# Score rows and A^T without TensorE in a two-layer graph kernel on Trainium2

## The chip, the cores and the metric

The kernel runs on one core of a Trainium2 chip. The metric is the device time of one execution in microseconds (us); the time before is the median of three runs. TensorE (PE) multiplies matrices and writes to PSUM. VectorE (DVE) and ScalarE (ACT) do elementwise work. GpSimd (POOL) and SyncE (SP) issue DMAs here; each engine runs its own instructions in order.

## What is computed

128 graphs of 128 nodes with 512 features each go through two layers; all data is float32. From the reference, shortened:

```python
h = maximum(layernorm(x), 0)                       # layer 0, X = h, A = adj
Xw = X @ Wv + bv
sj, si = Xw @ aw[:d, 0], Xw @ aw[d:, 0]
e = leaky_relu(sj[:, None, :] + si[:, :, None] + ab[0], 0.2)
alpha = A * exp(e)
T = alpha / (sum(alpha, axis=-1, keepdims=True) + 1e-12)
H = 0; Xk = X
for k in range(3):
    H = H + Xk @ Wk[k] + bk[k]
    Xk = einsum('bij,bjd->bid', T, Xk)
x = x + relu(H)

h = maximum(layernorm(x), 0)                       # layer 1
q, k = split(h @ Wqk, 2, axis=-1); v = h @ Wv
agg = einsum('bij,bjd->bid', adj, k * mask[:, :, None])
w = inv_scale * mask * einsum('bid,bid->bi', q, agg)
x = x + softmax(w, axis=1)[:, :, None] * v
```

## The kernel before, in words

**Tiles.** A round of the main loop handles two graphs (G = 2), so there are NP = 64 pairs. Nodes lie on the 128 partitions. `loads` holds x (`xg`) and the adjacency (`ag`), `front` and `late` the working tiles, `ps_m` four PSUM banks for the large products and `ps_t` four for everything else on TensorE.

**Layer 0** of pair p. `norm0` (L240) normalizes x into h; `by_blocks` (L258) writes h to DRAM (`hd`) and reads it back with its blocks exchanged (`hv`), so that VectorE's transpose, which turns blocks of 32x32, gives the whole transpose of h (`begin`, L447, by `transposed` L268). `score_sums` (L248) makes two dot products for each node, sj and si, by four VectorE operations with an accumulator (L255). `attention` (L274) needs sj along the free dimension, the same row on all partitions: `spread` (L95) lets TensorE transpose the column, broadcast to 128x128, into PSUM (L97). VectorE and ACT then make z, exp, the row sums and T (L280 to L294). TensorE also transposes A there (L298), and ACT scales it by the mask into `aT` (L302), for layer 1. `t_transposed` (L304) makes T^T on TensorE (L309), copies it, and multiplies it by T into (T^2)^T (L313). `propagate` (L317) gives T h and T^2 h in transposed form (L325). `prepare0` (L354) makes the sums of blocks that Strassen's scheme needs, and `strassen0` (L360) the product of [h, Th, T^2h] with the three weights in seven half-size products. They are called P1, P6, P7, P5, P2, P3, P4 here, in this order, by the first number in the calls of `product` (L340); each has 12 matmuls.

**Layer 1** of the pair before. `strassen1` (L387) multiplies h2 by a matrix of scores (Wq Wk^T) and by Wv in seven products of four matmuls, with the same names. It uses three PSUM banks a, b, c: P6 fills b, L398 reads b, and P5 writes b again. `aggregate` (L411) multiplies A by h2 (L417) and makes the scores w (L420). `finish` (L426) spreads w over the partitions as `attention` does (L97), makes the softmax over the nodes, scales v, adds it to x1 and stores the result.

**Order.** The main loop (L475 to L512) lets `strassen0` of pair p take in work of the next pair by two callbacks: `steps[0]` after P6 (begin, attention of p+1, finish of p-2) and `steps[1]` before P2 (t_transposed of p+1). After that come propagate of p+1, normalization of the new x1 into h2, strassen1 of p-1, aggregate of p-1, prepare0 of p+1, the transpose of h2 into X2, and last norm0 and score_sums of p+2. The code doesn't fix the order on an engine by itself: a scheduler sets it ahead of the run from the order of the code, which gives the priority, and from when it expects operands and buffers to be ready. On the chip each engine keeps that order and waits on semaphores. `h2` has one buffer, so a new h2 can be written only when A h2 of the pair before has read the old one.

Of the kernel before, what the change touches and what calls it, by code (L numbers as in the profile page):

```python
# [15 lines left out]
def kernel(  # L16
# [20 lines left out]
    nc = tc.nc  # L37
# [25 lines left out]

        return bass.AP(tensor=ap.tensor, offset=ap.offset + offset, ap=[[0, P], [1, n]])

    xg, ag = {}, {}

    def load(p):
        s = slice(p * G, (p + 1) * G)
        xg[p] = loads.tile([P, G, D], FP, name="xg")  # L70
        nc.sync.dma_start(xg[p], x[s].rearrange("b n d -> n b d"))
        ag[p] = loads.tile([P, G, N], FP, name="ag")
        nc.sync.dma_start(ag[p], adj[s].rearrange("b n m -> n b m"))


    nc.scalar.preload_act_table_set("natural_log_exp_and_others")
# [159 lines left out]
                                 bias=rs[:, 1, j:j + 1], scale=rs[:, 0, j:j + 1])  # L236
        return h

    H, HV, S, X, SX, AT, T, TT, X1, H2, X2, SX2 = ({} for _ in range(12))

    def norm0(p):

# [5 lines left out]
    def score_sums(p):  # L248

        h = H[p]  # L250
        s = S[p] = small.tile([P, G, 2], FP, name="s")
        for j in range(G):
            for a in range(2):
                junk = front.tile([P, D], FP, name="junk", bufs=1)
                nc.vector.scalar_tensor_tensor(junk, h[:, j, :], 1.0, u_bc[:, a, :], op0=OP.mult,  # L255
                                               op1=OP.mult, accum_out=s[:, j, a:a + 1])

    def by_blocks(h):  # L258

# [14 lines left out]
    def attention(p):  # L274

        a, s = ag.pop(p), S.pop(p)
        pz = ps_t.tile([P, DC, P], FP, name="pt")
        for j in range(G):
            spread(pz[:, j, :], s[:, j, 0:1])
        z = front.tile([P, G, N], FP, name="z", bufs=1)  # L280
        for j in range(G):
            nc.vector.tensor_scalar(z[:, j, :], pz[:, j, :], s[:, j, 1:2], cz, op0=OP.add, op1=OP.add)
# [9 lines left out]
        t = T[p] = front.tile([P, G, N], FP, name="t")  # L292
        for j in range(G):
            nc.vector.tensor_scalar(t[:, j, :], ex[:, j, :], d[:, 1, j:j + 1], None, op0=OP.mult)  # L294

        pa = ps_t.tile([P, DC, P], FP, name="pt")
        for j in range(G):
            nc.tensor.transpose(pa[:, j, :], a[:, j, :], ident)  # L298
        AT[p] = front.tile([P, G, N], FP, name="aT", bufs=3)
        for j in range(G):  # L300
            b = p * G + j
            nc.scalar.activation(AT[p][:, j, :], pa[:, j, :], AF.Copy, scale=maskT[:, b:b + 1])  # L302

    def t_transposed(p):  # L304

        t, tt = T.pop(p), front.tile([P, G, 2, N], FP, name="tt")
        pt = ps_t.tile([P, DC, P], FP, name="pt")
        for j in range(G):
            nc.tensor.transpose(pt[:, j, :], t[:, j, :], ident)  # L309
# [77 lines left out]
    def strassen1(p):  # L387
# [10 lines left out]
        nc.vector.tensor_add(s[:, 1], b, s[:, 0])  # L398
        product(c, 7, True)
        product(b, 5, False)  # L400
        nc.vector.tensor_add(s[:, 2], b, s[:, 0])
# [4 lines left out]
        nc.vector.tensor_add(o[0][1], b, s[:, 0])  # L406
        product(c, 4, False)
        nc.vector.tensor_add(o[1][0], c, s[:, 1])
        return yv

    def aggregate(p, yv):  # L411

        h2, at = H2.pop(p), AT.pop(p)
        w = small.tile([P, 6, G], FP, name="w")
        for j in range(G):
            pa = ps_t.tile([P, D], FP, name="pt")
            nc.tensor.matmul(pa, at[:, j, :], h2[:, j, :], start=True, stop=True)  # L417
            junk = front.tile([P, D], FP, name="junk", bufs=1)
            b = p * G + j
            nc.vector.scalar_tensor_tensor(  # L420
                junk.rearrange("p (k d) -> p k d", k=2), pa.rearrange("p (k d) -> p k d", k=2),
                wscale[:, b:b + 1], yv[:, j, :, 0, :], op0=OP.mult, op1=OP.mult,
                accum_out=w[:, 0, j:j + 1])
        return w

    def finish(p, yv, w):  # L426

        pw = ps_t.tile([P, DC, P], FP, name="pt")
        for j in range(G):
            spread(pw[:, j, :], w[:, 0, j:j + 1])  # L430
        nc.vector.tensor_reduce(w[:, 1], pw[:, :G, :], AX.X, OP.max, negate=True)
        for j in range(G):
            ej = front.tile([P, N], FP, name="ej")
            nc.scalar.activation(ej, pw[:, j, :], AF.Exp, bias=w[:, 1, j:j + 1],
                                 accum_out=w[:, 2, j:j + 1])
        nc.vector.tensor_add(w[:, 3], w[:, 0], w[:, 1])
# [32 lines left out]
    R1 = None  # L469
    ends = []  # L470

    def end():
        while ends:
            finish(*ends.pop())

    for p in range(NP + 1):
        if p < NP:
            if p + 1 < NP:
                n = p + 1
                steps = (lambda: (begin(n), attention(n), end()), lambda: t_transposed(n))  # L480
            else:
                steps = (end, lambda: None)
            strassen0(p, steps)
            if p + 1 < NP:
                propagate(p + 1)
# [52 lines left out]
```

## Time and profile before

| | us |
|---|---|
| median of 3 runs | 2419.33 (2419.09 to 2419.66) |
| the profiled execution, its own time | 2420.37 |
| its span in the trace | 2418.3 |
| one round of the loop (from P1 of layer 1 to the next) | 36.70 |
| start of the first product of layer 0 that runs without a break (P6) | 55.10 |
| start of the last pair's strassen1, after a wait of 6.5 us | 2394.32 |

A round has 84 matmuls of layer 0 (128x256, one every 0.216 us), 28 of layer 1 and four of A h2 (128x512, one every 0.429), 16 of propagate and twelve of 128x128 (one every 0.11): two transposes each of the z column, of A, of the w column and of T, and four for T^2. TensorE's granted clock is 1.00 in the loop. A row of the timeline gives start, duration, engine, line, operation, output and inputs, and the number of instructions merged into it; on TensorE the duration of a merged row contains the modelled end of the last, so the distance between starts is the better measure.

### The profile page before, as it was taken

The page shows a single profiled execution, that of the slowest core. Times are in us where ns is not written, and L with a number is a line of the kernel's source. Part 1 is how long each engine was busy: PE and PEld are TensorE (multiplying, and loading weights), DVE is VectorE, ACT ScalarE, POOL GpSimd, SP SyncE. Part 2 cuts the span into 40 slices and gives each one's busy share as a digit, 9 for nine tenths or more (in the row PEclk, how much of TensorE's full clock was granted, in tenths as well). Part 3 has the DMA queues.
Part 4 walks back from the last instruction along what each step waited for, and adds up shares of the span by engine and source line. Part 5 has one row for each costly group of instructions (what it writes and reads, how often), then busy time and mean ns, then how long its engine had stood idle before and what let it go on. Part 6 is the DMA issues. An engine that isn't in the chain of part 4 may idle for free.

```text
span 2418.3 us, 27245 instructions
## 1 busy us (share of the span) xinstructions
PE 2378.8 (98%) x9289; PEld 1694.5 (70%) x9289; DVE 1786.8 (74%) x4768; ACT 650.5 (27%) x1557; POOL 0.7 (0%) x6
## 2 busy tenths in 40 slices
PE   6999999999999999999999999999999999999997
PEld 4777677677676676776776776776766767767764
DVE  6777777777777777777777777777777777777764
ACT  3222222222222222223222222222222222232221
POOL 0000000000000000000000000000000000000000
PEclk9999999999999999999999999999999999999999
DMA  7233233233133233232332332332332332323311
GB/s 219 82 84 101 81 92 101 66 106 101 64 109 93 71 101 95 77 101 88 85 101 81 92 100 65 108 100 64 108 93 72 101 95 78 100 87 86 97 52 52
DMA packets 236986, 220.48 MB, mean 91 GB/s; under 512 B 14384, under 2 KB 170160, under 8 KB 236848
## 3 DMA queue, kind: packets, MB, share of 16 engines
q1 hardware_dynamic: 232624, 216.65, 30.5%
q10 hardware_dynamic: 4224, 2.10, 0.3%
q8 instruction: 73, 1.20, 0.2%
q14 instruction: 65, 0.53, 0.1%
HBM read 118.03 MB, written 100.66 MB: 90 GB/s over the span
## 4 chain that ended last, share of the span: by engine, by line
PE 96%; DVE 2%; DMA 1%; issue 0%; ACT 0%; SPq 0%; DVEq 0%; ACTq 0%
PE pm L346 79%; PE pt L325 9%; PE pt L417 4%; PE pt L97 1%; PE pt L313 1%; PE pt L298 1%; PE pt L309 1%; DMA bk_bc<-in_L_gnn_bk_dram 0%; DMA hd<-h 0%; DVE st L220 0%; DMA hv<-hd 0%; DMA w<-in_L_gnn_Wqk_dram 0%; DMA xg<-in_x_dram 0%; DVE x L271 0%; PE pm L208 0%
## 5 line engine op out<-in xcount | busy, mean ns | idle before, releaser
L346 PE MATMUL pm<-t,sx 128*128 128x256 f32 x2304 | 518.6, 380 | 1.4 <-DVE sx L333 1.4
L346 PEld LDWEIGHTS pm<-t,sx 128*128 128x128 f32 x2304 | 433.4, 190 | 57.4 <-DVE sx L333 2.0
L346 PE MATMUL pm<-b,x 128*128 128x256 f32 x1536 | 363.0, 380 | 0.0
L346 PE MATMUL pm<-f,sx 128*128 128x512 f32 x768 | 344.8, 598 | 0.3
L346 PEld LDWEIGHTS pm<-b,x 128*128 128x128 f32 x1536 | 282.6, 191 | 59.3 <-issue 29.6
L327 ACT COPY x<-pt 128x512 f32<-128x512 f32 x256 | 148.7, 581 | 500.6 <-PE pt L325 500.6
L346 PEld LDWEIGHTS pm<-f,sx 128*128 128x128 f32 x768 | 141.6, 191 | 193.7 <-issue 154.4
L346 PE MATMUL pm<-e,x 128*128 128x512 f32 x512 | 242.5, 596 | 6.5 <-DVE x L271 6.5
L325 PE MATMUL pt<-tt,h 128*128 128x256 f32 x1024 | 231.5, 379 | 0.0
L325 PEld LDWEIGHTS pt<-tt,h 128*128 128x128 f32 x1024 | 194.9, 190 | 26.2
L255 DVE SCALAR_TENSOR_TENSOR junk<-h,u_bc 128x512 f32<-128x512 f32 x256 | 176.4, 689 | 7.8 <-ACT h L235 0.9
L346 PE MATMUL pm<-b,sx 128*128 128x256 f32 x768 | 176.5, 379 | 0.0
L346 PE MATMUL pm<-t,x 128*128 128x256 f32 x768 | 176.2, 379 | 0.0
L235 ACT ACTIVATE h<-x,rs 128x512 f32<-128x512 f32 x128 | 97.2, 806 | 289.9 <-PE pt L417 277.1
L271 DVE STREAM_TRANSPOSE x<-hv 128x512 f32<-128x512 f32 x256 | 166.4, 688 | 6.6 <-DMA hv<-hd 5.7
L346 PEld LDWEIGHTS pm<-e,x 128*128 128x128 f32 x512 | 97.8, 191 | 102.8 <-issue 92.3
L346 PEld LDWEIGHTS pm<-t,x 128*128 128x128 f32 x768 | 146.2, 190 | 19.6
L346 PEld LDWEIGHTS pm<-b,sx 128*128 128x128 f32 x768 | 146.0, 190 | 19.5
L406 DVE TENSOR_TENSOR yv<-pm,s 128x512 f32<-128x512 f32 x64 | 44.3, 692 | 128.5 <-PE pm L346 128.5
L235 ACT ACTIVATE h<-xg,rs 128x512 f32<-128x512 f32 x128 | 97.2, 806 | 119.8 <-DVE rs L232 119.8
L417 PE MATMUL pt<-h,aT 128*128 128x512 f32 x256 | 120.5, 593 | 0.5 <-ACT h L235 0.5
L346 PE MATMUL pm<-e,sx 128*128 128x512 f32 x256 | 120.3, 592 | 0.0
(101 smaller groups left out, 2511.3 us busy)
## 6 DMA issues: line engine op xcount, KB each, us to landing
hd<-h SPq DMA_DIRECT2D x128, 512.0 KB, 3.1
hv<-hd SPq DMA_DIRECT2D x512, 128.0 KB, 3.3
xg<-in_x_dram SPq DMA_DIRECT2D x64, 512.0 KB, 3.6
out_dram<-x SPq DMA_DIRECT2D x64, 512.0 KB, 3.1
ag<-in_adj_dram SPq DMA_DIRECT2D x64, 128.0 KB, 3.0
w<-in_L_gnn_Wqk_dram ACTq DMA_DIRECT2D x8, 256.0 KB, 5.0
b<-in_L_gnn_Wk_dram SPq DMA_DIRECT2D x8, 256.0 KB, 3.4
wv_sb<-in_L_gnn_Wv_dram SPq DMA_DIRECT2D x4, 256.0 KB, 5.3
```

The costliest lines, as they stand in the source:

```text
L97: nc.tensor.transpose(dst, col.to_broadcast([P, P]), ident)
L235: nc.scalar.activation(h[:, j, :], src[:, j, :], AF.Relu, bias=rs[:, 1, j:j + 1], scale=rs[:, 0, j:j + 1])
L255: nc.vector.scalar_tensor_tensor(junk, h[:, j, :], 1.0, u_bc[:, a, :], op0=OP.mult, op1=OP.mult, accum_out=s[:, j, a:a + 1])
L271: nc.vector.transpose(dst[:, j].rearrange("p f (n b) -> p f n b", n=Q), hv[:, j].rearrange("p n (f a) -> p f n a", f=Q))
L298: nc.tensor.transpose(pa[:, j, :], a[:, j, :], ident)
L309: nc.tensor.transpose(pt[:, j, :], t[:, j, :], ident)
L313: nc.tensor.matmul(pt[:, j, :], t[:, j, :], tt[:, j, 0, :], start=True, stop=True)
L325: nc.tensor.matmul(pt[:, c].rearrange("p k n -> p (k n)"), h[:, j, at:at + P], tt[:, j].rearrange("p k n -> p (k n)"), start=True, stop=True)
L327: nc.scalar.copy(X[p][:, 1:3, j, kh].rearrange("p k c n -> p c k n"), pt)
L346: nc.tensor.matmul(bank[:, :r.shape[-1]], left[i][:, k, c * P:(c + 1) * P], r, start=(first and at == 0), stop=(at == len(chunks) - 1), sk ...
L406: nc.vector.tensor_add(o[0][1], b, s[:, 0])
L417: nc.tensor.matmul(pa, at[:, j, :], h2[:, j, :], start=True, stop=True)
```

## The change

- **A^T**: `load` also reads the adjacency by blocks (`agb`, four DMAs on GpSimd's queue, runs of 32 elements); VectorE's block transpose gives A^T in SBUF, and ACT scales it there. TensorE's two transposes go.
- **Score rows**: the sums are written into constant tiles of 32 columns (`cols`, six of them, zeroed once). `spread_pair` turns such a tile by VectorE's block transpose, writes two rows to DRAM and reads them back broadcast to all partitions, on GpSimd's queue. The sj row of pair 0 and the w row of the last pair still go by TensorE.
- **Order**: `strassen0` has three callbacks: begin after P6, attention after P7, t_transposed before P2; finish comes after that, with its maximum in a part of `s` that the sums before it use. A h2 of the two graphs lies inside strassen1, after P7 and after P2; the scores are made at its end. norm0 of p+2 comes before strassen1, and score_sums of p+2 inside it, after P5.
- **Buffers**: z, exp (now the same tile), t and tt have one buffer instead of two (z had one).

```diff
@@ load
+        agb[p] = loads.tile([P, G, Q, S32], FP, name="agb", bufs=2)
+        v = adj[s].rearrange("g (q b) (c i) -> c b (g q) i", b=S32, i=S32)
+        for c in range(Q):
+            nc.gpsimd.dma_start(agb[p][c * S32:(c + 1) * S32].rearrange("p g q i -> p (g q) i"), v[c])
@@ score_sums
+    cols = [const.tile([P, S32], FP, name=f"col{i}") for i in range(6)]
+    for t in cols:
+        nc.gpsimd.memset(t, 0.0)
...
-        s = S[p] = small.tile([P, G, 2], FP, name="s")
+        s = S[p] = cols[p % 3]
...
-                                               op1=OP.mult, accum_out=s[:, j, a:a + 1])
+                                               op1=OP.mult, accum_out=s[:, a * G + j:a * G + j + 1])
+        PZ[p] = spread_pair(s, "pz", p > 0)
@@ new
+    def spread_pair(col, name, by_dma):
+        if by_dma:
+            t = small.tile([P, S32], FP, name=f"{name}t", bufs=1)
+            nc.vector.transpose(t, col)
+            d = dram.tile([G, Q, S32], FP, name=f"{name}d")
+            for j in range(G):
+                nc.gpsimd.dma_start(d[j], t[j::S32])
+            dst = front.tile([P, G, N], FP, name=name, bufs=1)
+            nc.gpsimd.dma_start(dst.rearrange("p g n -> p (g n)"), bcast(d, 0, G * N))
+            return dst
+        pz = ps_t.tile([P, DC, P], FP, name="pt")
+        for j in range(G):
+            spread(pz[:, j, :], col[:, j:j + 1])
+        return pz[:, :G]
@@ attention
-        a, s = ag.pop(p), S.pop(p)
-        pz = ps_t.tile([P, DC, P], FP, name="pt")
-        for j in range(G):
-            spread(pz[:, j, :], s[:, j, 0:1])
+        a, s, pz = ag.pop(p), S.pop(p), PZ.pop(p)
...
-        ex = front.tile([P, G, N], FP, name="ex")
+        ex = z
...
-        pa = ps_t.tile([P, DC, P], FP, name="pt")
-        for j in range(G):
-            nc.tensor.transpose(pa[:, j, :], a[:, j, :], ident)
         AT[p] = front.tile([P, G, N], FP, name="aT", bufs=3)
+        nc.vector.transpose(AT[p].rearrange("p g n -> p (g n)"),
+                            agb.pop(p).rearrange("p g q i -> p (g q i)"))
...
-            nc.scalar.activation(AT[p][:, j, :], pa[:, j, :], AF.Copy, scale=maskT[:, b:b + 1])
+            nc.scalar.activation(AT[p][:, j, :], AT[p][:, j, :], AF.Copy, scale=maskT[:, b:b + 1])
@@ strassen0
         product(bc, 7, True)
+        steps[1]()
         product(bb, 5, False)
         nc.vector.tensor_add(s[:, 3], b, s[:, 0])
         nc.vector.tensor_add(hb[:, 1, HD:], c, s[:, 3])
-        steps[1]()
+        steps[2]()
+        end(s[:, 3, :G])
         product(ba, 2, False)
@@ strassen1
         product(c, 7, True)
+        agg = [aggregate(p, 0)]
         product(b, 5, False)
         nc.vector.tensor_add(s[:, 2], b, s[:, 0])
         nc.vector.tensor_add(o[1][1], c, s[:, 2])
+        if ahead < NP:
+            score_sums(ahead)
         product(a, 2, False)
         nc.scalar.copy(o[0][0], a)
+        agg.append(aggregate(p, 1))
+        H2.pop(p), AT.pop(p)
...
-        return yv
+        return yv, scores(p, yv, agg)
@@ aggregate is only the product now, scores has the rest; finish gets the row
-        pw = ps_t.tile([P, DC, P], FP, name="pt")
-        for j in range(G):
-            spread(pw[:, j, :], w[:, 0, j:j + 1])
-        nc.vector.tensor_reduce(w[:, 1], pw[:, :G, :], AX.X, OP.max, negate=True)
+        nc.vector.tensor_reduce(peak, pw, AX.X, OP.max, negate=True)
@@ main loop
-                steps = (lambda: (begin(n), attention(n), end()), lambda: t_transposed(n))
+                steps = (lambda: begin(n), lambda: attention(n), lambda: t_transposed(n))
...
+        if p + 2 < NP:
+            norm0(p + 2)
         if p > 0:
-            yv = strassen1(p - 1)
-            w = aggregate(p - 1, yv)
+            yv, w = strassen1(p - 1, p + 2)
+        elif p + 2 < NP:
+            score_sums(p + 2)
         if p + 1 < NP:
             prepare0(p + 1)
         if p > 0:
-            ends.append((p - 1, yv, w))
+            ends.append((p - 1, yv, w, spread_pair(w, "pw", p < NP)))
...
-        if p + 2 < NP:
-            norm0(p + 2)
-            score_sums(p + 2)
```

More of the change, by code (lines that the diff above doesn't have):

```diff
@@ L64, in bcast @@
         return bass.AP(tensor=ap.tensor, offset=ap.offset + offset, ap=[[0, P], [1, n]])
-    xg, ag = {}, {}
+    xg, ag, agb = {}, {}, {}
     def load(p):
@@ L237, in norm_relu @@
         return h
-    H, HV, S, X, SX, AT, T, TT, X1, H2, X2, SX2 = ({} for _ in range(12))
+    cols = [const.tile([P, S32], FP, name=f"col{i}") for i in range(6)]
+    for t in cols:
+        nc.gpsimd.memset(t, 0.0)
+    H, HV, S, PZ, X, SX, AT, T, TT, X1, H2, X2, SX2 = ({} for _ in range(13))
     def norm0(p):
@@ L272, in transposed, with attention @@
                                 hv[:, j].rearrange("p n (f a) -> p f n a", f=Q))
-    def attention(p):
-        a, s = ag.pop(p), S.pop(p)
+    def spread_pair(col, name, by_dma):
[8 more added lines that the diff above has]
+            return dst
         pz = ps_t.tile([P, DC, P], FP, name="pt")
         for j in range(G):
-            spread(pz[:, j, :], s[:, j, 0:1])
+            spread(pz[:, j, :], col[:, j:j + 1])
+        return pz[:, :G]
+    def attention(p):
+        a, s, pz = ag.pop(p), S.pop(p), PZ.pop(p)
         z = front.tile([P, G, N], FP, name="z", bufs=1)
         for j in range(G):
-            nc.vector.tensor_scalar(z[:, j, :], pz[:, j, :], s[:, j, 1:2], cz, op0=OP.add, op1=OP.add)
+            nc.vector.tensor_scalar(z[:, j, :], pz[:, j, :], s[:, G + j:G + j + 1], cz, op0=OP.add, op1=OP.add)
         nc.vector.scalar_tensor_tensor(z, z, 0.2, z, op0=OP.mult, op1=OP.max)
-        ex = front.tile([P, G, N], FP, name="ex")
+        ex = z
         nc.scalar.activation(ex, z, AF.Exp)
@@ L291, in attention @@
         nc.vector.reciprocal(d[:, 1], d[:, 0])
[L292 removed]
+        t = T[p] = front.tile([P, G, N], FP, name="t", bufs=1)
         for j in range(G):
             nc.vector.tensor_scalar(t[:, j, :], ex[:, j, :], d[:, 1, j:j + 1], None, op0=OP.mult)
[L296 to L298 removed]
         AT[p] = front.tile([P, G, N], FP, name="aT", bufs=3)
+        nc.vector.transpose(AT[p].rearrange("p g n -> p (g n)"),
+                            agb.pop(p).rearrange("p g q i -> p (g q i)"))
         for j in range(G):
             b = p * G + j
[L302 removed]
+            nc.scalar.activation(AT[p][:, j, :], AT[p][:, j, :], AF.Copy, scale=maskT[:, b:b + 1])
     def t_transposed(p):
[L306 removed]
+        t, tt = T.pop(p), front.tile([P, G, 2, N], FP, name="tt", bufs=1)
         pt = ps_t.tile([P, DC, P], FP, name="pt")
@@ L385, in strassen0, with strassen1 @@
                                            op0=OP.max, op1=OP.add)
-    def strassen1(p):
+    def strassen1(p, ahead):
         product = products(SX2.pop(p), R1)
@@ L408, in strassen1, with aggregate, scores @@
         nc.vector.tensor_add(o[1][0], c, s[:, 1])
-        return yv
-    def aggregate(p, yv):
-        h2, at = H2.pop(p), AT.pop(p)
-        w = small.tile([P, 6, G], FP, name="w")
+        return yv, scores(p, yv, agg)
+    def aggregate(p, j):
+        pa = ps_t.tile([P, D], FP, name="pt")
+        nc.tensor.matmul(pa, AT[p][:, j, :], H2[p][:, j, :], start=True, stop=True)
+        return pa
+    def scores(p, yv, agg):
+        w = cols[3 + p % 3]
         for j in range(G):
-            pa = ps_t.tile([P, D], FP, name="pt")
-            nc.tensor.matmul(pa, at[:, j, :], h2[:, j, :], start=True, stop=True)
             junk = front.tile([P, D], FP, name="junk", bufs=1)
@@ L420, in aggregate, with finish @@
             nc.vector.scalar_tensor_tensor(
-                junk.rearrange("p (k d) -> p k d", k=2), pa.rearrange("p (k d) -> p k d", k=2),
+                junk.rearrange("p (k d) -> p k d", k=2), agg[j].rearrange("p (k d) -> p k d", k=2),
                 wscale[:, b:b + 1], yv[:, j, :, 0, :], op0=OP.mult, op1=OP.mult,
-                accum_out=w[:, 0, j:j + 1])
+                accum_out=w[:, j:j + 1])
         return w
-    def finish(p, yv, w):
-        pw = ps_t.tile([P, DC, P], FP, name="pt")
-        for j in range(G):
-            spread(pw[:, j, :], w[:, 0, j:j + 1])
-        nc.vector.tensor_reduce(w[:, 1], pw[:, :G, :], AX.X, OP.max, negate=True)
+    def finish(peak, p, yv, ws, pw):
+        w = ws[:, :6 * G].rearrange("p (k g) -> p k g", g=G)
+        nc.vector.tensor_reduce(peak, pw, AX.X, OP.max, negate=True)
         for j in range(G):
             ej = front.tile([P, N], FP, name="ej")
-            nc.scalar.activation(ej, pw[:, j, :], AF.Exp, bias=w[:, 1, j:j + 1],
+            nc.scalar.activation(ej, pw[:, j, :], AF.Exp, bias=peak[:, j:j + 1],
                                  accum_out=w[:, 2, j:j + 1])
-        nc.vector.tensor_add(w[:, 3], w[:, 0], w[:, 1])
+        nc.vector.tensor_add(w[:, 3], w[:, 0], peak)
         nc.scalar.activation(w[:, 4], w[:, 3], AF.Exp)
@@ L470, with end @@
     ends = []
-    def end():
+    def end(peak=None):
         while ends:
-            finish(*ends.pop())
+            finish(small.tile([P, G], FP, name="peak") if peak is None else peak, *ends.pop())
     for p in range(NP + 1):
@@ L479 @@
                 n = p + 1
-                steps = (lambda: (begin(n), attention(n), end()), lambda: t_transposed(n))
+                steps = (lambda: begin(n), lambda: attention(n), lambda: t_transposed(n))
             else:
-                steps = (end, lambda: None)
+                steps = (lambda: None,) * 3
             strassen0(p, steps)
```

## The prediction

> **What bounds the kernel now.** I read the page's busy times and the chain of waits first, then the windows of one round of the loop, then the timeline of that round on TensorE and VectorE. The first fence has the page's busy times, the chain's shares by engine and one row of the windows (one round: us, then busy time of PE, PEld, DVE, ACT and POOL, clock, DMA share, GB/s).
>
> ```profile
> PE 2378.8 (98%) x9289; PEld 1694.5 (70%) x9289; DVE 1786.8 (74%) x4768; ACT 650.5 (27%) x1557; POOL 0.7 (0%) x6
> PE 96%; DVE 2%; DMA 1%; issue 0%; ACT 0%; SPq 0%; DVEq 0%; ACTq 0%
> 1017.43:1054.13 36.70, 36.70 (x146) 26.26 (x145) 27.58 (x75) 10.01 (x25) 0.00 (x0) 1.00 0.30 90
> ```
>
> TensorE is busy for all of the 36.70 us of a round, and 96% of the chain is TensorE. So in the loop a matmul taken out is time gained, and work added to DVE (27.58 of 36.70), ACT or POOL costs nothing until TensorE has to wait for it. The next fence is the timeline of TensorE around the place concerned (start us, us).
>
> ```profile
> 1033.65 2.75 PE L346 MATMUL pm<-t,sx 128*128 128x256 f32 x12
> 1036.24 0.38 PE L97 MATMUL pt<-ident,s 128*128 128x128 f32 x2
> 1036.46 0.38 PE L298 MATMUL pt<-ident,ag 128*128 128x128 f32 x2
> 1036.68 0.38 PE L97 MATMUL pt<-ident,w 128*128 128x128 f32 x2
> 1036.90 5.35 PE L346 MATMUL pm<-t,sx 128*128 128x256 f32 x24
> 1042.08 0.38 PE L309 MATMUL pt<-ident,t 128*128 128x128 f32 x2
> ```
>
> P6 of layer 0 starts at 1033.65; then come the six transposes that the change removes, P7 and P5 in one row, and T^T. The true cost of a row is the distance to the next start: the six transposes take 1036.90 - 1036.24 = 0.66 us, 0.11 each (the printed 0.38 contains a pipelined end). Next the waits (us, times, longest), and VectorE's timeline of the same round.
>
> ```profile
> PEld pm L346 <- DVE s L398: 38.8, 63, 1.0
> ACT h L235 <- PE pt L417: 277.1, 61, 4.6
> ...
> 1024.40 0.69 DVE L401 TENSOR_TENSOR s<-pm,s 128x512 f32<-128x512 f32 x1 [1.15 <-PE pm L346]
> 1027.83 0.69 DVE L406 TENSOR_TENSOR yv<-pm,s 128x512 f32<-128x512 f32 x1 [2.01 <-PE pm L346]
> 1029.55 0.69 DVE L408 TENSOR_TENSOR yv<-pm,s 128x512 f32<-128x512 f32 x1 [1.02 <-PE pm L346]
> 1034.56 0.68 DVE L255 SCALAR_TENSOR_TENSOR junk<-h,u_bc 128x512 f32<-128x512 f32 x1
> 1036.79 0.72 DVE L282 TENSOR_SCALAR z<-pt,s,cz 128x128 f32<-128x128 f32 x2
> 1040.22 0.48 DVE L294 TENSOR_SCALAR t<-ex,d 128x128 f32<-128x128 f32 x2
> ```
>
> The last score sum starts at 1034.56, z at 1036.79, and T is complete at 1040.22 + 0.48 = 1040.70, while T^T starts at 1042.08: T is 1.4 us early. VectorE idles 1.15, 2.01 and 1.02 us during layer 1's products. Last, the page's landing times, which I use for the new transfers:
>
> ```profile
> hd<-h SPq DMA_DIRECT2D x128, 512.0 KB, 3.1
> hv<-hd SPq DMA_DIRECT2D x512, 128.0 KB, 3.3
> ```
>
> **What the Trainium skill says.** "TensorE: Matmul & The Clock Gate", Part 4, says that TensorE's transpose does a full 128x128 but leaves it in PSUM, for another engine to copy out; the trace agrees (L298, then ACT L302 out of pt). "VectorE: DVE Perf Modes", "The three transpose paths", says that DVE transposes 32x32 blocks only; this is why the change loads A a second time with its blocks exchanged, and the kernel's L271 already works so. "DMA: Bandwidth & Descriptors", "Anatomy of one DMA", prices a DMA issued by GpSimd at about 2.0 us plus bytes over 436 GB/s; no row of this trace shows one. "SBUF — State Buffer", "SBUF: two separate sides", warns that GpSimd can't write descriptors while VectorE runs an operation in a two-port mode; nothing here shows whether that matters.
>
> **The change part by part.**
>
> *Transposes removed.* Of six in a round, the pair for z stays in round 0 (one of 64), the pair for w in the last (one of 64), the pair for A^T never: 2 x 63 + 2 x 63 + 2 x 64 = 380. 380 x 0.11 = 41.8 us, all on TensorE. The few in the prologue and the tail may lie beside idle TensorE; that is under 1 us.
>
> *A h2 between layer 1's products.* The four matmuls (0.43 each) move, none is added. Now P5 waits for L398's reading of the bank that P6 filled. The listed wait is 38.8 us, but most of it lies in the 0.24 that the weight loads always show: from P6's start (1018.99) to P2's (1024.20) are 5.21 us for 12 x 0.429 = 5.15. So 0.06 us a round; 0.86 us of A h2 between P7 and P5 covers it: 63 x 0.06 = 3.8 us gained.
> The same move frees h2 early: ACT writes the next h2 only when A h2 has read the old one (277.1 us of waits). In the loop this gains nothing, as X2 is ready long before layer 1 needs it. In the last round it does: h2 was written at 2384.84 and strassen1 waited for it through hd, hv and L271 until 2394.32. A h2 of the round before now ends after P2 (some 10.5 us after 2370.90, so 2381.4): 3.4 us earlier, and with it the end.
>
> *Work added on VectorE and ACT.* One block transpose of 128x256 (about 0.42, as L332 of that size: 425 ns; L271 is 688 for twice that), two of 128x32 (0.16 each, as L231). z and the maximum read SBUF instead of PSUM: z between 280 (L294) and 402 ns each. So +0.5 to +0.75 us of DVE, 28.3 of 36.0. The A^T scaling on ACT stays 363 ns or so. Cover: TensorE's 36 us; nothing of it is charged.
>
> *The score row by DMA.* Now: sums, TensorE, z in 1.5 us. After: sums, block transpose, two small GpSimd writes to DRAM, a broadcast back, z. Two transfers one after the other, from 2 x 2.0 + 0.3 = 4.3 us (estimate after the DMA page) to 6.4 (hd plus hv), or more if GpSimd takes its time over descriptors. I take 6.5 with the block transpose. Deadline: P1 still starts at 1031.06; P7 and P5 end 0.66 earlier than now, so T is needed at 1041.4. The chain z to T took 1036.79 to 1040.70, 3.9 us, with 1.6 us of finish between it; finish now comes later, but the A^T transpose and begin's two (0.69 each) may fall there. So z has to start by 1037.5 and the sums to end by 1031.0. Now they end at 1035.2; the change calls them inside strassen1, after P5's additions. h is ready by 1024.8 (ACT L235 at 1023.28 plus 1.52), and the gaps of VectorE above (4.2 us) hold the four sums (0.69 and 0.08 each, 3.1): end about 1029, row there at 1035.5, two us in hand. Queued behind z on VectorE are everything to T, s3 and the output sums; behind T, TensorE.
>
> *The score row of the other layer* (w): sums end at 1032.1, row there at about 1039. Only finish needs it, and its maximum is written over s[:,3], so it can't be placed before P5's sums (1042.7): cover 3 us.
>
> *norm0 and its DMAs.* h's hd and four hv on SP go from the round's end to before strassen1. They were issued at 1032.81 together with h2's, since SP stood waiting for h2; that wait falls 3.4 us. xg and ag wait for the same buffers as now. POOL's queue in order: four loads of A by blocks, the z row, the w row. The loads need the buffer that attention frees early in the round, some 20 us before the z row wants POOL. Their 1,024 runs of 128 B and 0.26 MB of broadcast rows raise the DMA share from 0.30 to about 0.4: no queue fills.
>
> *Single buffers for z, t, tt (ex is z).* Each is rewritten a round after its last reader: nothing.
>
> *Prologue.* More transfers at the start, and the rows of rounds 1 and 2 go through DRAM when there is no lead yet: 0 to 8 us, I take 3.
>
> Sum against the profiled execution (2420.37, span 2418.3): -41.8 - 3.8 - 3.4 + 3 = -46.0, 2374.4. The median of the runs shown is 1.0 lower: 2373.
>
> **The rivals.**
> A (forecast), 2373. All the cover holds. Own range 2364 (nothing lost in the prologue, small idle times gone) to 2386.
> B, gain partly given back: VectorE is crowded between P6 and T^T (X2's transposes and sums, 2.7 us, may now come before T), T 0.4 us late, 62 x 0.4 = 25: 2398. For: T had only 1.4 us; against: 3.1 us of sums and 2.4 us of finish leave that stretch.
> C, all given back: T 0.7 late, 2417.
> D, slower: the z row lands after z's place. VectorE stands at z, T is late, TensorE waits at T^T every round. It decides from 0.73 us of lateness, since a round gains 0.66 + 0.06. If each of the two GpSimd transfers takes 1.75 us more than SP's, the 2 us in hand turn into 1.5 us late: 62 x 1.5 = 93, less 46: 2466. If the sums stayed where they are (end 1035.2), it would be 4 us: some 2620. For: no row shows a GpSimd transfer, and there are two in series; against: VectorE's gaps.
> E, that the change doesn't do it: the order on each engine is fixed ahead by a scheduler, not the code (begin's transposes, first in the code, run at 1013.52, as P4 ends). It can put products before T^T when it expects T late; that softens B and D and is within A.
>
> **How the numbers follow.** A 0.58, B 0.12, C 0.06, D 0.24. Within 0.2% (4.8 us) is what a measurement of this kernel can't tell from no change. Faster: A and B, 0.70; same: C, 0.06; slower: D, 0.24. The range goes from A's lower end, 2364, to 2445, the near part of D (1.15 us late); what is left out is D's far part and a little below A, 0.2. A's own range is 2364 to 2386.
>
> **What would show it.** A round of 35.97 us with TensorE busy throughout; no L97 or L298 row in it; T complete before T^T without a wait; the z row on POOL issued by about 1029 and landed by 1037. Wrong: a wait of DVE z on a DMA, TensorE idle before T^T, POOL's instructions of more than 2 us in a row, or idle time moved to layer 1's first product.

## The result: slower, and where the profile after puts the time

The changed kernel takes 2536.94 us (median of six runs, 2531.15 to 2545.13) against 2419.67 for the kernel before: ratio 1.0487, 95% interval 1.0469 to 1.0505. The forecast of 2373, and its range up to 2445, are wrong. The profiled execution, the slowest of the six, took 2545.13 us with a span of 2543.4. Where its 125.1 us more than the span before lie, from the starts of strassen1 in both traces:

| stretch | before, us | after, us | difference |
|---|---|---|---|
| start, to strassen1 of pair 1 | 136.13 | 151.10 | +15.0 |
| 60 rounds, to strassen1 of pair 61 | 2202.69 | 2309.74 | +107.0 |
| the rest | 79.48 | 82.56 | +3.1 |

A round takes 38.50 us in the mean in place of 36.71. The shortest take 35.99, which is close to the forecast's 35.97; the longest takes 43.1. So the shorter round exists, and something late spoils most rounds, by an amount that varies. First the page's busy times and one long round in the windows (us, then busy time of PE, PEld, DVE, ACT and POOL, clock, DMA share, GB/s):

```profile
PE 2387.1 (94%) x8909; PEld 1658.1 (65%) x8909; DVE 1803.9 (71%) x4958; ACT 631.9 (25%) x1557; POOL 369.6 (15%) x646
```

```profile
1034.00:1072.86 38.86, 36.78 (x139) 25.45 (x138) 28.24 (x79) 9.65 (x24) 5.82 (x10) 1.00 0.37 96
```

TensorE has 380 matmuls fewer and is no longer busy throughout: 36.78 of 38.86 us. VectorE's 28.24 is what the forecast had (28.3), so it isn't too busy; it stands still at the wrong moment. The waits (us in total, times, longest) say at which one:

```profile
PE pm L367 <- DVE s L390: 79.2, 54, 3.3
PE pm L367 <- DVE s L421: 22.7, 22, 2.9
...
PEld pm L367 <- DVE s L390: 103.0, 60, 3.7
PEld pm L367 <- DVE s L421: 57.1, 48, 3.8
...
DVE z L304 <- DMA pz<-pzd: 249.0, 63, 5.3
DVE s L461 <- DMA pw<-pwd: 79.7, 51, 4.2
```

VectorE stands at z (L304) in all 63 rounds until the row has landed, 249.0/63 = 4.0 us each time. TensorE then stands at a product of layer 0 (L367, the line of every product) that waits for L390, and at one of layer 1 that waits for L421. L390 makes s2 from P6: it reads the bank that P6 filled and that P5 fills next. L421 does the same in layer 1, and L425 there reads P5's bank. PE and PEld show the same stops, so the two aren't added. The timeline of the round shows how z and L390 hang together:

```profile
1043.40 0.69 DVE L262 SCALAR_TENSOR_TENSOR junk<-h,u_bc 128x512 f32<-128x512 f32 x1
1044.62 0.20 DVE L287 STREAM_TRANSPOSE pzt<-col 128x32 f32<-128x32 f32 x1
1045.11 1.11 POOL L290 DMA_DIRECT2D pzd<-pzt  x2 [22.36 <-DVE pzt L287]
1046.21 1.22 POOL L77 DMA_DIRECT2D agb<-in_adj_dram  x2
1048.29 2.75 PE L367 MATMUL pm<-b,x 128*128 128x256 f32 x12
1049.12 0.58 POOL L292 DMA_DIRECT2D pz<-pzd  x1 [1.69 <-issue]
1050.88 5.34 PE L367 MATMUL pm<-t,sx 128*128 128x256 f32 x24
1054.73 0.35 DVE L304 TENSOR_SCALAR z<-pz,col,cz 128x128 f32<-128x128 f32 x1 [4.75 <-DMA pz<-pzd]
1054.99 0.20 DVE L287 STREAM_TRANSPOSE pwt<-col 128x32 f32<-128x32 f32 x1
1057.41 0.48 DVE L316 TENSOR_SCALAR t<-z,d 128x128 f32<-128x128 f32 x2
1057.81 0.42 DVE L390 TENSOR_TENSOR s<-pm,s 128x256 f32<-128x256 f32 x1
1058.28 2.86 PE L367 MATMUL pm<-t,sx 128*128 128x256 f32 x12 [2.05 <-DVE s L390]
1060.97 0.38 PE L330 MATMUL pt<-ident,t 128*128 128x128 f32 x2
```

P1 starts at 1048.29, P6 and P7 at 1050.88 in one row, P5 at 1058.28 after 2.05 us of idle time. On VectorE all of attention, from z to T, stands ahead of L390, though the code has L390 first: the order on the engine is the scheduler's. From z's start to L390's end are 3.50 us (1054.73 to 1058.23), and P7 ends 36 x 0.216 = 7.78 us after P1's start. So z has to start by 4.28 us after P1; here it starts 6.44 after. T^T at 1060.97 finds T complete since 1057.89. TensorE doesn't wait there. The block transpose of the w row (pwt, 1054.99) stands behind z as well, so that this row sets out late too.

The page's landing times have the other half (KB each, median us from issue to landing):

```profile
hd<-h SPq DMA_DIRECT2D x128, 512.0 KB, 4.0
hv<-hd SPq DMA_DIRECT2D x512, 128.0 KB, 6.3
...
agb<-in_adj_dram POOLq DMA_DIRECT2D x256, 32.0 KB, 4.9
pz<-pzd POOLq DMA_DIRECT2D x63, 128.0 KB, 6.0
pw<-pwd POOLq DMA_DIRECT2D x63, 128.0 KB, 3.3
```

The z row needs 6.0 us and the w row, of the same shape, 3.3. The read of h's blocks (hv), which took 3.3 us before, needs 6.3. The z row is issued at 1049.12 and hv from 1049.64 on: they are in flight together. hv is 1 MB a round, for h and h2 together.

### The profile page after: what moved, and what is told of

It is laid out like the page before. It is cut to its first block, busy times and chain, and to the rows that moved or that the text cites. A ratio compares the mean times of both kernels' runs of the same rounds, so it can differ in the third digit from the quotient of the medians.

```text
span 2543.4 us, 27641 instructions
## 1 busy us (share of the span) xinstructions
PE 2387.1 (94%) x8909; PEld 1658.1 (65%) x8909; DVE 1803.9 (71%) x4958; ACT 631.9 (25%) x1557; POOL 369.6 (15%) x646
## 5 line engine op out<-in xcount | busy, mean ns | idle before, releaser
L367 PE MATMUL pm<-t,sx 128*128 128x256 f32 x2304 | 535.8, 388 | 80.9 <-DVE s L390 79.2
L367 PEld LDWEIGHTS pm<-t,sx 128*128 128x128 f32 x2304 | 440.6, 193 | 164.7 <-DVE s L390 103.0
L367 PE MATMUL pm<-f,sx 128*128 128x512 f32 x768 | 357.4, 601 | 22.9 <-DVE s L421 22.7
L367 PE MATMUL pm<-b,x 128*128 128x256 f32 x1536 | 363.2, 380 | 0.0
L367 PEld LDWEIGHTS pm<-b,x 128*128 128x128 f32 x1536 | 282.9, 191 | 59.7 <-issue 29.7
L367 PEld LDWEIGHTS pm<-f,sx 128*128 128x128 f32 x768 | 143.5, 191 | 219.0 <-issue 144.8
L290 POOL DMA_DIRECT2D pzd<-pzt x126 | 69.9, 556 | 1431.2 <-DVE pzt L287 1421.7
L367 PE MATMUL pm<-e,x 128*128 128x512 f32 x512 | 245.2, 602 | 13.9 <-DVE x L279 13.9
L304 DVE TENSOR_SCALAR z<-pz,col,cz 128x128 f32<-128x128 f32 x126 | 41.0, 327 | 249.0 <-DMA pz<-pzd 249.0
L367 PE MATMUL pm<-t,x 128*128 128x256 f32 x768 | 176.2, 379 | 0.0
L367 PE MATMUL pm<-b,sx 128*128 128x256 f32 x768 | 176.2, 379 | 0.0
L367 PEld LDWEIGHTS pm<-e,x 128*128 128x128 f32 x512 | 98.7, 193 | 112.9 <-issue 93.6
L367 PEld LDWEIGHTS pm<-t,x 128*128 128x128 f32 x768 | 145.9, 190 | 19.8
L367 PEld LDWEIGHTS pm<-b,sx 128*128 128x128 f32 x768 | 145.9, 190 | 19.8
L307 ACT ACTIVATE z<-z 128x256 f32<-128x256 f32 x64 | 26.7, 417 | 520.0 <-DVE z L305 520.0
L77 POOL DMA_DIRECT2D agb<-in_adj_dram x256 | 152.9, 602 | 16.6 <-DVE aT L319 10.0
```

Source lines behind the costliest of these rows:

```text
L77: nc.gpsimd.dma_start(agb[p][c * S32:(c + 1) * S32].rearrange("p g q i -> p (g q) i"), v[c])
L290: nc.gpsimd.dma_start(d[j], t[j::S32])
L304: nc.vector.tensor_scalar(z[:, j, :], pz[:, j, :], s[:, G + j:G + j + 1], cz, op0=OP.add, op1=OP.add)
L367: nc.tensor.matmul(bank[:, :r.shape[-1]], left[i][:, k, c * P:(c + 1) * P], r, start=(first and at == 0), stop=(at == len(chunks) - 1), sk ...
```

## Experiments

Three causes were to be told apart: *place* (z stands ahead of L390 on VectorE), *contention* (the row's transfer is slowed by what runs beside it), and *queue* (GpSimd issues ten transfers a round, six for the rows and four loads of A, one after the other).

### s2's addition ahead of z

```diff
...
+            czp = small.tile([P, 1], FP, name="czp")
+            nc.vector.scalar_tensor_tensor(czp, after, 0.0, cz, op0=OP.mult, op1=OP.add)
...
-            nc.vector.tensor_scalar(z[:, j, :], pz[:, j, :], s[:, G + j:G + j + 1], cz, op0=OP.add, op1=OP.add)
+            nc.vector.tensor_scalar(z[:, j, :], pz[:, j, :], s[:, G + j:G + j + 1], czp, op0=OP.add, op1=OP.add)
...
-        steps[1]()
+        steps[1](s[:, 2, 0:1])
...
```

`after` is a column of s2, so that z can't be ordered ahead of L390; the value stays cz.

> The changed kernel with one more VectorE instruction of 128x1 in attention (cz plus 0 times a column of s2), which z then reads, so that z and all behind it can't stand ahead of the addition of s2 on VectorE. Theory 'place': P5 of layer 0 waits because s2 (L390) is queued behind z, which waits for its row. Then the wait of TensorE on s2 (79 us) goes, the w row (queued behind z too) comes some 4 us earlier, and the waits of layer 1 (L421, L425, some 50 us together) shrink with it: 2385 to 2420 us. Theory 'landing': the row comes too late for T^T too; then TensorE waits at T^T about as long as it did at P5, and the time stays over 2480.

Measured: 2396.84 us against 2420.0 before (0.9903, 0.9886 to 0.992): 140 us less than the changed kernel, by one tiny operation a round. The timeline, where L394 is s2's addition:

```profile
1023.37 2.75 PE L371 MATMUL pm<-b,x 128*128 128x256 f32 x12
1025.96 7.93 PE L371 MATMUL pm<-t,sx 128*128 128x256 f32 x36
1028.75 0.42 DVE L394 TENSOR_TENSOR s<-pm,s 128x256 f32<-128x256 f32 x1 [1.83 <-PE pm L371]
1029.41 0.60 DVE L308 TENSOR_SCALAR z<-pz,col,czp 128x128 f32<-128x128 f32 x2
1031.90 0.48 DVE L320 TENSOR_SCALAR t<-z,d 128x128 f32<-128x128 f32 x2
1033.73 0.38 PE L334 MATMUL pt<-ident,t 128*128 128x128 f32 x2
```

P6, P7 and P5 run as one row of 36. z starts 6.04 us after P1, later than the 5.75 that the changed kernel has in the median, and T is still complete 1.35 us ahead of T^T. The row itself lands 5.1 us after P1 (median; 5.7 in the changed kernel), still past 4.28. The median round is 35.98. *Place* holds: a z that starts so late is harmless where nothing that TensorE needs sooner is queued behind it. The dependence also lets the w row's block transpose go ahead of z: it starts 1.72 us after P1 in place of 6.02 (medians), and the weight loads' waits for layer 1's two additions fall from 57.1 and 39.5 us to 18.7 and 22.0. So the 140 us are not L390's alone.

### GpSimd's queue, and the loads of A

The A block's loads moved to SP's queue, all else as changed:

```diff
...
-            nc.gpsimd.dma_start(agb[p][c * S32:(c + 1) * S32].rearrange("p g q i -> p (g q) i"), v[c])
+            nc.sync.dma_start(agb[p][c * S32:(c + 1) * S32].rearrange("p g q i -> p (g q) i"), v[c])
```

> The changed kernel with the four loads of A by blocks on SP's queue instead of GpSimd's. Theory 'queue': these loads of 128 B runs stand in the same queue before and behind the z row and delay it; then the broadcast of the z row lands in about 3.3 us as that of the w row does, instead of 6.0, and the time falls to 2450 to 2490. Theory 'bulk': what delays it are the 2 MB of hd and hv on SP's queue that are under way at the same moment; then it still takes 5 us or more, and the time stays at 2510 to 2560.

Measured: 2503.46 us (1.0353, 1.0335 to 1.037), between the two ranges. The row still needs 5.4 us to land, as 'bulk' had it, and TensorE still waits for L390:

```profile
PE pm L367 <- DVE s L390: 85.9, 59, 3.4
...
PEld pm L367 <- DVE s L421: 3.0, 7, 0.7
```

The row isn't issued sooner: 0.30 us after P1 in the median, where the changed kernel has it 0.47 ahead. *Queue* isn't what makes z late. The 33 us gained lie for the most part in layer 1: the waits for L421 and L425 are all but gone, with z as late as before (5.70 after P1). So the loads of A on GpSimd's queue do have a part in that second loss; the finish waits 44.2 us for its w row in place of 79.7. Whether it is their place in the queue or their traffic isn't shown.

A^T by TensorE again, without the loads of A by blocks, rows as changed:

```diff
...
-            nc.gpsimd.dma_start(agb[p][c * S32:(c + 1) * S32].rearrange("p g q i -> p (g q) i"), v[c])
...
-        nc.vector.transpose(AT[p].rearrange("p g n -> p (g n)"),
-                            agb.pop(p).rearrange("p g q i -> p (g q i)"))
+        pa = ps_t.tile([P, DC, P], FP, name="pt")
+        for j in range(G):
+            nc.tensor.transpose(pa[:, j, :], a[:, j, :], ident)
...
```

> The changed kernel with A^T made by TensorE as before, without the loads by blocks; the score rows still go through DRAM. Theory 'bulk' or 'place': the waits stay, and 128 transposes come back: about 2550, and no less than 2525. Theory 'queue': without the loads by blocks the rows land early, and the time falls to 2440 to 2490 in spite of the transposes.

Measured: 2449.2 us (1.0128, 1.011 to 1.0146), 88 us less although TensorE has 128 x 0.11 = 14 us more to do. That is the range of 'queue', far below what the other two expected. The row's landing falls only to 5.0 us, though, and hv's to 4.2; the sums end 0.6 us earlier against P1, and z starts 4.16 us after it in the median (5.75 in the changed kernel). Of these 1.6 us, 0.5 come from an earlier issue and 1.1 from the time between issue and z. The edit takes away the issues, the traffic and a VectorE operation at once, so it can't tell *queue* from *contention* by itself.

### A h2 back behind layer 1

```diff
...
-        agg = [aggregate(p, 0)]
...
-        agg.append(aggregate(p, 1))
...
+        agg = [aggregate(p, j) for j in range(G)]
...
```

> The changed kernel with A h2 of the round set back behind both of layer 1's product groups, so that the h2 write and its broadcast read are issued about 3.5 us later again; the score rows and A^T stay as changed. Theory 'contention' (the h2 read, 2 MB on SP's queue, beside the score row slows the row's landing): the row lands 3.3 to 4.5 us after its issue in place of 6.0, and the time falls below 2480 us. Theory 'place' (the row is late for VectorE's order of work whatever runs beside it): the row's landing stays at 5 to 6 us and the time stays between 2520 and 2560.

Measured: 2454.55 us (1.015, 1.0129 to 1.0171), as *contention* expected. (The expectation says 2 MB for the read; by the page it is 1 MB.) z still stands ahead of L390 on VectorE, but the wait for L390 is all but gone:

```profile
PE pm L367 <- DVE s L390: 6.4, 3, 3.2
...
PEld pm L367 <- DVE s L421: 69.4, 57, 2.4
PEld pm L367 <- DVE s L424: 49.8, 61, 0.9
...
DVE z L304 <- DMA pz<-pzd: 69.6, 63, 5.1
DVE s L460 <- DMA pw<-pwd: 95.3, 59, 2.8
```

```profile
hv<-hd SPq DMA_DIRECT2D x512, 128.0 KB, 3.7
...
pz<-pzd POOLq DMA_DIRECT2D x63, 128.0 KB, 3.3
pw<-pwd POOLq DMA_DIRECT2D x63, 128.0 KB, 4.5
```

With hd and hv issued later, the z row lands in 3.3 us and hv in 3.7. hd, the write of 1 MB, is under way beside the row here (issued 0.8 us after it in the median); the read hv comes only 4.7 us after the row's issue, when the row has landed. In the changed kernel it comes 1.45 after. So the write alone doesn't slow the row; the read does, or both together. Now the w row is the slow one (4.5), and the finish waits for it. The windows show what stood in the row's way. From its issue to z's start, first in the changed kernel, then here (columns as above):

```profile
1049.12:1054.73 5.61, 5.61 (x27) 4.94 (x27) 0.82 (x3) 0.00 (x0) 1.75 (x3) 1.00 0.90 214
```

```profile
1057.07:1060.41 3.34, 3.34 (x18) 2.93 (x17) 1.23 (x6) 1.28 (x3) 3.24 (x6) 1.00 0.51 152
```

The share of the 16 DMA engines is 0.90 at 214 GB/s while the row is under way in the changed kernel, 0.51 here (medians over the rounds, from issue to landing: 0.91 and 0.49); over the whole round it was 0.37. VectorE is busy for only 0.82 of the 5.61 us, so it isn't VectorE's work that slows the transfer. Times after P1's start, medians of 58 rounds:

| us after P1's start | sums end | row issued | z starts | z after issue |
|---|---|---|---|---|
| changed kernel | -4.20 | -0.47 | 5.75 | 6.22 |
| A h2 back | -2.76 | 0.99 | 4.37 | 3.38 |

GpSimd's part, sums to issue, is 3.7 us in both. The whole difference from the sums to z is the flight. The fall of L390's wait has a second cause, though: the order on VectorE is another one here.

```profile
1060.41 0.60 DVE L304 TENSOR_SCALAR z<-pz,col,cz 128x128 f32<-128x128 f32 x2 [0.82 <-DMA pz<-pzd]
1062.39 0.42 DVE L390 TENSOR_TENSOR s<-pm,s 128x256 f32<-128x256 f32 x1
1063.12 0.48 DVE L316 TENSOR_SCALAR t<-z,d 128x128 f32<-128x128 f32 x2
```

L390 stands ahead of T, and z's start to L390's end are 2.39 us in place of 3.49 (medians). So z is due 5.4 us after P1, and 4.37 keeps that with 1 us to spare. An estimate from these medians: in the changed kernel L390 ends 5.75 + 3.49 - 7.78 = 1.5 us late; the earlier row alone leaves 0.1 of it, the other order alone 0.4. So this run shows contention in the landing, but the time that it gained can't be put down to the landing alone.

### One row each by TensorE

z by TensorE at attention's place, w by transfers; then the reverse, w by TensorE in finish; then the latter with A h2 back as well:

```diff
...
-        PZ[p] = spread_pair(s, "pz", p > 0)
+        PZ[p] = s
...
-        a, s, pz = ag.pop(p), S.pop(p), PZ.pop(p)
+        a, s, pz = ag.pop(p), S.pop(p), spread_pair(PZ.pop(p), "pz", False)
```

```diff
-            ends.append((p - 1, yv, w, spread_pair(w, "pw", p < NP)))
+            ends.append((p - 1, yv, w, w))
...
+        pw = spread_pair(pw, "pw", False)
         nc.vector.tensor_reduce(peak, pw, AX.X, OP.max, negate=True)
```

> The changed kernel with the score row z by TensorE at attention's place, and the w row still by GpSimd's transfers. If the z row alone carries the loss: 2385 to 2400 (the floor of 36.0 a round and 0.2 for two spreads). If the w row has a loss of its own, as the waits on it at the finish and at layer 1's additions say: above 2405, at most 2440.

> The changed kernel with the w row by TensorE at the finish, and the z row still by GpSimd's transfers. GpSimd has three transfers a round less, so the z row should land sooner, but it still stands ahead of s2's addition beside the h2 read: 2440 to 2500. If the z row alone carries the loss it stays above 2520.

> A h2 back behind layer 1's products, as in the run in which the z row landed after 3.3 us, and the w row by TensorE. There the h2 read fell beside the w row (4.5 us to land) and VectorE was late for layer 1's additions. If that was the rest of the loss, the rounds fall to 36.2 to 36.5 and the time to 2385 to 2405. If layer 1's additions are late for another reason: 2430 to 2455.

Measured: 2404.84 (0.994, 0.9925 to 0.9955), 2445.19 (1.0106, 1.0088 to 1.0125) and 2418.52 us (0.9996, 0.9988 to 1.0004). The first fell between its two ranges: its rounds are even, 36.38, and no product waits for L390 or L421. So here the w row makes nothing late. But a late z alone does not make the loss at L421: with z late it is gone both in the second run (0.8 us), where the w row goes by TensorE, and with the loads of A on SP. It needs the w row by transfers and something that holds this row up. The first run also gains almost nothing against both rows by TensorE (36.42, below): T^2 now waits for ACT's copy of T^T (18.9 us, 61 times, 0.3 each). The second still loses by the z row (landing 5.4, 201.7 us of waits at z), though its median round is 36.52. The third's rounds are 36.38, but for one of 42.4, and so within what was expected of them; the time missed both of its ranges by that one round and by the start, 8.7 us longer than before's (144.85 to 136.13). Layer 1's additions still come late there (L424 45.0 us over 61 rounds, on the weight loads).

The landings of hv complete the picture: 3.6 us with the z row by TensorE (first), 5.5 with the z row by transfers beside it (second), 3.5 with the two apart (third). The row and the read slow each other.

### The other parts alone

Both rows by TensorE, first right behind the sums, then at the places of attention and finish; A^T by blocks, A h2 and the order stay as changed:

```diff
-        PZ[p] = spread_pair(s, "pz", p > 0)
+        PZ[p] = spread_pair(s, "pz", False)
...
-            ends.append((p - 1, yv, w, spread_pair(w, "pw", p < NP)))
+            ends.append((p - 1, yv, w, spread_pair(w, "pw", False)))
```

The second has both edits of the section before.

> The changed kernel with both score rows made by TensorE in every round; A^T by blocks, A h2 between the products, and the new order of norm0 and finish stay. If the loss is all in the score rows' way through DRAM: 128 transposes of A less (14 us), 4 us for A h2 and up to 4 in the tail, so 2395 to 2412, faster than before. If a part of it is in the loads by blocks, the moved A h2 or the order: 2430 or more.

> Both score rows are spread by TensorE again as before the change, at the places of attention and of the row's end; A^T by block transposes, A h2 between layer 1's products and T^T ahead of P2 stay as changed. If the parts other than the rows give what the sum of the prediction says (A^T's 128 small transposes 14 us, A h2's wait 4, the end 3): 2396 to 2406. If these parts are worth nothing beside the rows: 2415 to 2425.

Measured: 2432.38 us (1.0051, 1.0036 to 1.0066) and 2401.68 (0.9928, 0.9911 to 0.9944). The first lies in the range for a loss outside the rows, but the lines say otherwise: TensorE stands at the spread, right behind the sums.

```profile
PEld pt L101 <- DVE junk L262: 54.9, 64, 2.2
...
PE pt L101 <- DVE junk L262: 19.8, 61, 1.9
```

The second is in the range that the prediction's own sum gave, with even rounds of 36.42. So the loss was in the spread's place; A^T by blocks, A h2 and the order lose nothing.

The kernel before with A h2 alone moved:

```diff
...
         product(c, 7, True)
+        agg = [agg1(p, 0)]
...
         nc.scalar.copy(o[0][0], a)
+        agg.append(agg1(p, 1))
...
```

> The kernel before with A h2 alone moved between layer 1's two product groups. By the prediction's terms (3.8 us for the waits on the residual, 3.4 us at the end): 2410 to 2415. If the wait only comes back at the next use: 2418 to 2422. If A h2 there holds up layer 1's second products: over 2425.

Measured: 2412.07 us (0.9969, 0.9958 to 0.9981).

```profile
1014.37:1051.01 36.64, 36.64 (x146) 26.30 (x144) 27.21 (x75) 9.62 (x25) 0.00 (x0) 1.00 0.34 91
```

The round is 0.06 us shorter than before, and the stretch from strassen1 of pair 61 to the end 76.13 us in place of 79.48.

### The version that beats both

s2's addition ahead of z, the loads of A on SP, and the w row of the last pair but one by TensorE, as the first experiment's end had waited for it (10.2 us before the last strassen1):

```diff
...
-            ends.append((p - 1, yv, w, spread_pair(w, "pw", p < NP)))
+            ends.append((p - 1, yv, w, spread_pair(w, "pw", p < NP - 1)))
```

> The first experiment (the score row's use held behind s2's addition on VectorE) with two more edits: the A block's loads are issued by SP and not by GpSimd, and the w row of the last pair but one goes through TensorE, so that the end of the program does not wait for its transfer. Theory 'chain of transfers': GpSimd's queue is shorter by two issues a round, the rows land sooner, the few waits that were left go, and the end is some 5 us shorter: 2376 to 2390. If the loads on SP push the h2 write and read back instead, A h2's use waits and the time is 2395 or more.

Measured: 2379.67 us against 2419.4 (0.9835, 0.9821 to 0.985). The page's busy times and the windows of a round:

```profile
PE 2334.8 (98%) x8911; PEld 1659.6 (70%) x8911; DVE 1812.1 (76%) x5020; ACT 657.5 (28%) x1557; POOL 210.7 (9%) x387
```

```profile
1004.93:1040.91 35.98, 35.98 (x139) 25.70 (x138) 28.09 (x79) 10.16 (x25) 3.36 (x6) 1.00 0.40 103
```

TensorE is busy for all of 35.98 us, although z's row still needs 5.8 us to land. Against the span before: the start +5.2, 60 rounds -42.4, the end -3.2.

The first round of this version takes 40.7 us. Whether pair 1's row causes that:

```diff
-        PZ[p] = spread_pair(s, "pz", p > 0)
+        PZ[p] = spread_pair(s, "pz", p > 1)
```

> The combined version of the run before (row's use behind s2's addition, A block loads by SP, last w row by TensorE) with the first round's score row by TensorE too. In that version the first round took 40.7 us and all later ones 36.0. If the first row's late transfer is what makes it long, the first round falls to 36 to 37 and the time by 3 to 5 us, to 2374 to 2378. If something else of the start is late, the time stays at 2379 to 2381.

Measured: 2382.89 us (0.9847, 0.9832 to 0.9862); the first round is 41.9. Not the row, then. In the best version's trace this round holds, between layer 1's products, T^T, T^2 and propagate of pair 1: 4.1 us of matmuls that otherwise lie ahead of it. So its length is for the most part work counted in another place. The start's +5.2 is idle time: TensorE's waits up to the end of this round are 29.5 us in the best version and 23.4 in the kernel before. Which of the edits brings them stays open.

## Why the prediction was wrong

**Right: the transposes.** 0.11 us each, and the round of 35.97 that follows, are the 35.99 of the shortest rounds here and the 35.98 of nearly every round of the best version. With rows by TensorE and the rest changed, a round gains 0.28 (36.70 to 36.42), which is A^T's 0.22 and A h2's 0.06.

**Right: A h2 in itself.** 0.06 a round and 3.4 at the end were forecast; the kernel before with this part alone shows 0.06 and 3.35.

**Right: the work added on VectorE and ACT costs nothing,** as long as its order puts nothing urgent behind a wait: the best version has VectorE 76% busy and TensorE 98%. POOL's issues took 552 to 587 ns each for the z row; the lockout that "SBUF — State Buffer", "SBUF: two separate sides", warns of shows in none of them.

**Wrong: the step "The score row by DMA", at two points.** It takes both for the loss at L390: z late, and L390 queued behind it.

The first is its size, "I take 6.5 with the block transpose". From the sums' end to z it was 9.95 us in the median. The sums ended earlier than I had them (4.2 us ahead of P1, not 2.1), but z could start only 5.75 after P1 where the forecast had the row 4.4 after. With A h2 back it took 7.13 and z started 4.37 after. I had priced the transfers as if each flew alone, and under "norm0 and its DMAs" I argued "no queue fills" from a share of 0.4 over a whole round. While the row is in flight the share is 0.90. The same paragraph counted SP's earlier issue of hd and hv as harmless ("that wait falls 3.4 us"): that is what put 1 MB of reads beside the row, the hv of h and h2. "DMA: Bandwidth & Descriptors", "Issuing engines are not separate DMA queues", says that transfers run on the same 16 engines whichever engine issued them; the landings above agree (hv 3.3 to 6.3 us, the row 3.3 to 6.0). Its section "Anatomy of one DMA" would give the 128 KB row 2.3 us (estimate: 2.0 and 131072 bytes over 436 GB/s); the shortest landing of it here was 3.1, so for this transfer the measured time is the price to take.

The second is the deadline. "Queued behind z on VectorE are everything to T, s3 and the output sums" left out s2's addition, which the scheduler put behind attention too and which P5 waits for. I took T^T as the first to be late and had z due 6.4 us after P1; with L390 behind it, z was due 4.28 after. In the first experiment the old deadline was restored, and z, no earlier (6.04), made TensorE wait for neither L390 nor T^T.

**Wrong too: the cover of the other row.** "Only finish needs it" took the w row to be there 7.9 us after P1 (1039 in the trace before) and gave it 3 us of cover. It landed 15.45 after (median). Its block transpose stood behind z on VectorE, 6.02 after P1, which the step had not looked at. VectorE waited 79.7 us for the row at the finish, and layer 1's additions came late after that, the waits for L421 and L425.

**The rival D** had the right mechanism, a row that lands after z's place, and a wrong place: it said TensorE waits at T^T. Its own price followed from that deadline and came to 2466. Of the forecast's signs of being wrong, the wait of z on a DMA came; TensorE idle before T^T did not, as it stood one product earlier. E ("it can put products before T^T") looked at the scheduler for relief; here its order made the loss.

**The terms at the ends.** "I take 3" for the start was 15.0 in the changed kernel and 5.2 in the best one. The end's -3.4 became +3.1: h2 of the last pair was early, but its block transposes stood on VectorE behind the finish of the pair before, which waited 7.4 us for its w row. With that row by TensorE the end gained 3.2.

What stays open: how much of the 88 us that A^T by TensorE brought is traffic and how much order on VectorE; how the loads of A on GpSimd's queue make layer 1's additions late; what makes the start longer; and why the scheduler orders attention ahead of L390, which no trace shows.

## What to carry to other kernels

When a value comes to an in-order engine by a transfer, list everything that the scheduled order puts behind the first instruction that waits for it, and take as deadline the earliest need of any of these, not that of the value's own consumer. Price the transfer by the DMA share in the few us of its flight, after the change has moved the other transfers, and not by the mean of a round. If the landing can't be made early, one artificial dependence that lets the urgent work go first may be worth more than a faster transfer: here 140 us. And when an edit makes a wait shorter, look whether the scheduled order changed with it before the gain is put down to the transfer.

## What the hardware showed unexpectedly

- A broadcast of 1 KB from DRAM to 128 partitions (128 KB written) and the 1 MB read of h's blocks slow each other down to nearly half speed: 3.3 and 3.7 us to land apart, 6.0 and 6.3 together. The write of the same 1 MB (hd) beside the row does not: with A h2 back it was under way for most of the row's 3.3 us.
- Two rows of 512 B each written to DRAM took 1.6 us to land for z and 4.5 for w. The share of the DMA engines was 0.02 while z's were under way and 0.69 for w's (medians in the changed kernel): here small transfers paid for their neighbours as the large ones did.
- Moving A h2, which is worth 0.06 us a round on TensorE, cost 82 us in the changed kernel (2454.55 to 2536.94), by the transfers that it brought forward and by another order on VectorE.
